# A four-layer selective-scan kernel: delta u B of every fourth state on GpSimd, with B broadcast from DRAM and the decay in PSUM

## The chip, the cores and the metric

One core of one Trainium2 chip. The time is the device time of one launch in microseconds. The engines are called by the profile's names: PE (TensorE), with PEld for its weight loads, DVE (VectorE), ACT (ScalarE), POOL (GpSimd) and SP (SyncE, which here issues the DMAs).

## The reference

Four blocks of a vision state-space model, each `x = x + block(groupnorm(x))`, over 8 images of 48 x 48 positions (L = 2304) and 96 channels. In a block, a projection to 192 channels, a depthwise 3 x 3 convolution and silu give u. u is scanned in four directions (k: along rows, along columns, and both reversed), with 16 states n for each channel:

```
x_dbl = x_proj[k] @ xs[k]                       # -> dts, Bs (16 rows), Cs (16 rows)
delta = softplus(dt_proj[k] @ dts + bias)
dA    = exp(delta * A[n])
h     = dA * h + (delta * u) * B[n]             # a recurrence over the 2304 positions
y     = sum over n of h * C[n],  plus D * u
```

The four directions are summed, layer-normalised, multiplied by silu(z) and projected back to 96 channels. The last block forms the same recurrence from a cumulative sum of log dA, with dB u divided by (decay + 1e-12).

## The kernel before

The 8 images are handled as 4 pairs. The channels of a pair, 2 x 192, fill three tiles of 128 partitions: t = 0 and 1 are the first 128 channels of each image, t = 2 has the last 64 of both. For one layer and pair there are 12 groups (t, ph, d): three tiles, two scan layouts ph (rows, columns), two directions d. `prologue` makes u and the projections, which go to DRAM: `xd` holds the rows of dts, B and C in fp32, `xb` holds B split into three bf16 parts. `prepare` makes delta (`dl`) and delta times u (`du`) of one group, in five pieces. `epilogue` does the norm and the output projection in 16 pieces, `ECHUNKS`.

A group is scanned in three chunks of 768 positions, each with 16 states. One state of one chunk is a unit; the first three layers have 6912 of them. For a unit, class `Chunk` issues:

- `load`: broadcasts C's row of this state from `xd` to all partitions, tile `cb` (7 buffers); with the first state also the bf16 rows `brow`. All DMAs are on SP's queue.
- `decay`: `da = exp(A delta)` on ACT (L543), tile `da`, 4 buffers.
- `spread`: PE multiplies `brow` with a selecting matrix, which puts B's row on all partitions, in a PSUM tile `b` of two buffers (L558).
- `scan`: DVE multiplies `b` by `du` (L570), then scans `h = da * h + b` in place of `da` (L574). ACT keeps the last column for the next chunk (L585), and POOL multiplies C by h in place of `cb` (L586).
- `add_up`: PE adds that to the sum over states in PSUM with an identity matmul (L593); after state 15 `collect` adds the sum to `y`.

The order of the work is written out in `run`, for unit k of the list `todo`: make the next unit ready, scan this one, take one step of the generators that run beside it (`prepare` of the next group, `prologue` of the next pair in the last third of a pair, `epilogue` of the previous pair in the first two thirds), and add up the unit three before:

```
get_ready(k + 1)
c.scan(n)
step(coming)
...
todo[k - LAG][1].add_up(todo[k - LAG][2])      # LAG = 3
```

`get_ready(k)` loads C of unit k + 2 (`LOADS`), makes the decay of unit k + 1 (`DECAYS`) and spreads B of unit k. The framework beneath puts in the semaphores, gives out the buffers of a tile's pool, and may move an instruction ahead of others on its engine where its own timing model has it ready first; so the order on an engine is near the written one, but not it.

The last layer is scanned by class `Edge` on its outer rows alone, four states at a time, by the same calls `load`, `decay`, `spread`, `scan`, `add_up`.

Of the kernel before, what the change touches and what calls it, by code (L numbers as in the profile page):

```python
# [31 lines left out]
F32 = mybir.dt.float32  # L35
# [4 lines left out]
P = 128  # L40
# [3 lines left out]
NS = 16  # L44
# [48 lines left out]
def ss2d_layers_kernel(ctx: ExitStack, tc: tile.TileContext, x_in, consts, weights, out):  # L93
# [7 lines left out]
    ypool = ctx.enter_context(tc.tile_pool(name="y", bufs=1))  # L101
    rpool = ctx.enter_context(tc.tile_pool(name="brow", bufs=2))
    cbpool = ctx.enter_context(tc.tile_pool(name="cb", bufs=7))
    apool = ctx.enter_context(tc.tile_pool(name="da", bufs=4))
    qpool = ctx.enter_context(tc.tile_pool(name="rq", bufs=2))
    capool = ctx.enter_context(tc.tile_pool(name="carry", bufs=2))
    tmp = ctx.enter_context(tc.tile_pool(name="tmp", bufs=3))
# [399 lines left out]
    class Chunk:  # L507


        def __init__(self, l, p, t, ph, d, i, group):  # L510
            self.l, self.p, self.t, self.ph, self.d, self.group = l, p, t, ph, d, group
            self.c0, self.m = SCANS[i if d == 0 else len(SCANS) - 1 - i]
            self.first, self.last = i == 0, i == len(SCANS) - 1
            self.batches = range(2) if t == 2 else (t,)
            self.brow = self.acc = None
            self.cb, self.da, self.rq, self.b, self.h = {}, {}, {}, {}, {}

        def load(self, n):

# [16 lines left out]

        def decay(self, n):

            s, m = state[self.l, self.p], self.m
            dl, _ = s["dd", self.t, self.ph, self.d]  # L540
            da = apool.tile([P, SCAN], F32, name="da", tag="da")[:, :m]
            self.da[n] = da
            nc.scalar.activation(  # L543
                da, dl[:, self.c0 : self.c0 + m], AF.Exp,
                scale=columns_of(self.l, self.t, self.ph, self.d, n),
            )

        def spread(self, n):

            if self.l == NLAYER - 1:  # L550

                self.rq[n] = rq = qpool.tile([P, SCAN], F32, name="rq", tag="rq")[:, : self.m]
                nc.scalar.activation(rq, self.da[n], AF.Ln, bias=decay_eps)
                nc.scalar.activation(rq, rq, AF.Exp, scale=-1.0)
            k, w = picked(self.t, n)
            self.b[n] = b = pb.tile([P, 2 * BANK], F32, name="b", tag="b")
            for z, zm in pieces(self.m):
                nc.tensor.matmul(  # L558
                    b[:, z : z + zm], w, self.brow[:k, z : z + zm], start=True, stop=True
                )  # L560

        def scan(self, n):
            s, m = state[self.l, self.p], self.m
            way = (lambda z: z) if self.d == 0 else (lambda z: z[:, ::-1])
            _, du = s["dd", self.t, self.ph, self.d]
            carries = self.group["carry"]
            start = 0.0 if self.first else carries[:, n : n + 1]
            da, c = self.da.pop(n), self.cb[n][:, :m]
            b = self.b.pop(n)[:, :m]
            nc.vector.tensor_mul(b, du[:, self.c0 : self.c0 + m], b)  # L570
            if self.l < NLAYER - 1:

                h = da
                nc.vector.tensor_tensor_scan(way(h), way(da), way(b), start, ALU.mult, ALU.add)  # L574
# [11 lines left out]
            nc.gpsimd.tensor_mul(c, c, h)  # L586
# [38 lines left out]
    class Edge:  # L625
# [10 lines left out]
        @staticmethod  # L636
        def quad(z, pitch=EDGE):
            return z[:, : QUAD * pitch].rearrange("p (n m) -> p n m", n=QUAD)[:, :, :EDGE]

        def load(self, i):  # L640
            s = state[self.l, self.p]
# [86 lines left out]
    def epilogue(l, p):  # L728
# [110 lines left out]
    def run(pairs, short):  # L839
# [22 lines left out]

        def get_ready(k):

            if k == 0:
                for i in range(LOADS):
                    todo[i][1].load(todo[i][2])
                for i in range(DECAYS):
                    todo[i][1].decay(todo[i][2])
            if k + LOADS < len(todo):  # L870
                todo[k + LOADS][1].load(todo[k + LOADS][2])
            if k + DECAYS < len(todo):
                todo[k + DECAYS][1].decay(todo[k + DECAYS][2])
# [157 lines left out]
```

## Time and profile before

| what | value |
|---|---|
| median of 3 runs | 25,898.13 us (25,891.26 to 25,907.81) |
| profiled run | 25,884.7 us; its span 25,882.9 us |
| granted PE clock, mean | 0.881 |
| DMA | 3150.92 MB, 122 GB/s, 40.2% of 16 engines' span |

A profile is of one execution. In its lines "L570 DVE ... b<-du,b" is line 570 of the kernel, the engine, and the tile written and the tiles read; "x6912 | 6481.8, 951" the count, the busy time in us and the mean of one in ns; then the idle time of the engine just before these instructions, and what ended it ("<-PE b L558 2461.6"). Lines of waits have the waiting instruction, the one that released it, and the time in us in all, the number of times and the longest. The three regular layers take the first 23,700 us of the span, the last layer the rest.

### The profile page before, as it was taken

What the parts mean: (1) busy time and instruction counts of PE and PEld (TensorE: products, weight loads), DVE (VectorE), ACT (ScalarE), POOL (GpSimd) and SP (SyncE); (2) the same over time, 40 slices, a digit from 0 to 9 for tenths busy, and PEclk for the clock granted to TensorE, in tenths of its full rate; (3) what the DMA queues carried; (4) which work ended last, traced back from release to release, by engine and by line L of the source; (5) the groups of instructions that cost most, each with busy time, mean ns of one, the idle gap of its engine ahead of it and who ended that gap; (6) DMA issues with size and microseconds to landing.
All of it is one profiled execution on the core that took longest, in us unless ns stands there. A gap on an engine that the chain in (4) does not pass through costs nothing. (4 is left out here: it accounts for less than half of the span.)

```text
span 25882.9 us, 233918 instructions
## 1 busy us (share of the span) xinstructions
PE 20983.2 (81%) x64962; PEld 9542.0 (37%) x64962; DVE 20922.0 (81%) x18566; ACT 13772.3 (53%) x22878; POOL 15340.0 (59%) x9545
## 2 busy tenths in 40 slices
PE   7787887887887887887887887887887887887886
PEld 2333333333333333333333333333333333334555
DVE  5888888988888988988988988988888988887443
ACT  4454554554554554554554554554554554555775
POOL 4656656656666656656656656656656656655332
PEclk8898898998898898898898998898898998898886
DMA  2344444434434444434434444444434434444221
GB/s 90 126 122 130 132 123 127 134 119 130 134 120 132 135 121 133 134 121 134 134 121 131 134 122 130 134 121 130 134 119 132 134 120 130 132 122 115 64 62 50
DMA packets 1463442, 3150.92 MB, mean 122 GB/s; under 512 B 190832, under 2 KB 563696, under 8 KB 1448944
## 3 DMA queue, kind: packets, MB, share of 16 engines
q1 hardware_dynamic: 1462128, 3135.85, 40.2%
q8 instruction: 525, 8.60, 0.1%
q14 instruction: 789, 6.46, 0.1%
HBM read 2971.05 MB, written 164.07 MB: 121 GB/s over the span
## 5 line engine op out<-in xcount | busy, mean ns | idle before, releaser
L586 POOL TENSOR_TENSOR cb<-cb,da 128x768 f32<-128x768 f32 x6912 | 12427.8, 1809 | 7755.9 <-DVE da L574 4843.6
L593 PE MATMUL acc<-cb,cst 128*128 128x512 f32 (+1 forms) x27648 | 12228.8, 568 | 2394.0 <-POOL cb L586 2114.9
L543 ACT ACTIVATE da<-dl,a 128x768 f32<-128x768 f32 x6912 | 6448.9, 935 | 7878.0 <-POOL cb L586 7851.1
L570 DVE TENSOR_TENSOR b<-du,b 128x768 f32<-128x768 f32 x6912 | 6481.8, 951 | 2488.9 <-PE b L558 2461.6
L574 DVE TENSOR_TENSOR_SCAN da<-da,carry,b 128x768 f32<-128x768 f32 x4608 | 8182.2, 1801 | 90.0 <-ACT da L543 35.4
L593 PEld LDWEIGHTS acc<-cb,cst 128*128 128x128 f32 x27648 | 5323.8, 213 | 7776.8 <-issue 4049.3
L558 PE MATMUL b<-brow,pick 48*128 48x512 bf16 (+3 forms) x13824 | 3721.7, 354 | 1719.3 <-DVE da L574 1637.9
L574 DVE TENSOR_TENSOR_SCAN da<-da,b 128x768 f32<-128x768 f32 x2304 | 3961.5, 1742 | 83.1 <-ACT da L543 54.1
L558 PEld LDWEIGHTS <-pick 48*128 48x128 bf16 (+1 forms) x13824 | 919.9, 98 | 5287.6 <-DVE da L574 3139.0
L585 ACT COPY carry<-da 128x1 f32<-128x1 f32 x4608 | 847.4, 184 | 2226.7 <-DVE da L574 2205.3
L258 PE MATMUL ps<-pad,diag 128*128 128x480 f32 (+1 forms) x4320 | 1799.7, 559 | 60.2 <-ACT u L223 36.3
L461 POOL TENSOR_TENSOR lg<-lg,w 128x480 f32<-128x480 f32 (+2 forms) x768 | 864.8, 1126 | 837.5 <-ACT w L459 753.6
L464 DVE SCALAR_TENSOR_TENSOR ps<-ps,lg 128x480 f32<-128x480 f32 (+2 forms) x768 | 473.9, 617 | 799.3 <-POOL lg L462 756.3
L258 PEld LDWEIGHTS ps<-pad,diag 128*128 128x128 f32 x4320 | 783.2, 191 | 857.9 <-issue 619.9
L444 PE MATMUL ps<-dts,w 6*128 6x480 f32 (+8 forms) x2048 | 933.3, 628 | 73.9 <-DVE du L470 39.5
L744 PE MATMUL ps<-ey,cst 128*128 128x144 f32 (+1 forms) x4096 | 846.9, 334 | 82.4 <-ACT ey L768 66.5
L462 POOL TENSOR_TENSOR lg<-lg,e 128x480 f32<-128x480 f32 (+2 forms) x768 | 863.0, 1124 | 37.3
L745 PE MATMUL ps<-ey,mean 128*128 128x144 f32 (+1 forms) x4096 | 782.7, 315 | 0.0
L744 PEld LDWEIGHTS ps<-ey,cst 128*128 128x128 f32 (+1 forms) x4096 | 511.6, 179 | 364.9 <-issue 185.3
L448 ACT ACTIVATE ps<-ps,w 128x480 f32<-128x480 f32 (+2 forms) x768 | 457.7, 596 | 347.4 <-PE ps L444 346.8
L224 ACT ACT_TABLE_LOAD x496 | 636.4, 1283 | 8.7
L223 ACT ACT_TABLE_LOAD x496 | 636.4, 1283 | 8.2
(118 smaller groups left out, 14292.6 us busy)
## 6 DMA issues: line engine op xcount, KB each, us to landing
cb<-xd SPq DMA_DIRECT2D x4736, 384.0 KB
cb<-xd SPq DMA_DIRECT2D x4736, 192.0 KB
yd<-y SPq DMA_DIRECT2D x48, 1152.0 KB
ey<-yd SPq DMA_DIRECT2D x256, 216.0 KB
brow<-xb SPq DMA_DIRECT2D x576, 72.0 KB
xb<-parts SPq DMA_DIRECT2D x288, 108.0 KB
ex<-xs SPq DMA_DIRECT2D x256, 108.0 KB
xd<-xt SPq DMA_DIRECT2D x32, 684.0 KB
```

Source lines behind the costliest of these rows:

```text
L258: nc.tensor.matmul(ps[:, :m], ly.diag[:, int(t == 2), j, :], pad[:, r0 + dy : r0 + dy + nr, dx : dx + W], start=(j == 0), stop=(j == 8),)
L444: nc.tensor.matmul(o[:, :m], ly.dtw[q0 : q0 + r, k, chans], dts[q0 : q0 + r, :m], start=True, stop=True,)
L461: nc.gpsimd.tensor_sub(lg, lg, w1)
L462: nc.gpsimd.tensor_add(lg, lg, e)
L543: nc.scalar.activation(da, dl[:, self.c0 : self.c0 + m], AF.Exp, scale=columns_of(self.l, self.t, self.ph, self.d, n),)
L558: nc.tensor.matmul(b[:, z : z + zm], w, self.brow[:k, z : z + zm], start=True, stop=True)
L570: nc.vector.tensor_mul(b, du[:, self.c0 : self.c0 + m], b)
L574: nc.vector.tensor_tensor_scan(way(h), way(da), way(b), start, ALU.mult, ALU.add)
L585: nc.scalar.copy(carries[:, n : n + 1], h[:, end : end + 1])
L586: nc.gpsimd.tensor_mul(c, c, h)
L593: nc.tensor.matmul(self.acc[:, z : z + zm], ident, c[:, z : z + zm], start=(n == 0), stop=(n == NS - 1),)
L744: nc.tensor.matmul(o, mean_w[:, cols], z[:, b, :], start=True, stop=False)
```

## The change

In the first three layers, every fourth state (n = 3, 7, 11, 15) becomes a pooled one. For such a unit:

- B's row comes in fp32 from `xd` by a broadcasting DMA, as C's does, into a new SBUF tile `bb` of two buffers. This `load_b` is issued four units ahead (`LOADS + 2`).
- POOL multiplies it by `du` in place (`weigh`), one unit ahead.
- `spread` issues no matmuls. Instead the exp of the decay is made there, and it is written to a PSUM tile of the pool that the others use for B.
- `scan` has no multiplication on DVE; the scan reads the decay from PSUM and `bb` from SBUF and writes h to `bb`, which POOL and ACT then read.

The other units stay as they were. The decay of an unpooled unit is now issued after the spread of the unit before it. `da` has 3 buffers where it had 4, and `ex` and `ey` of the epilogue have one where they had two. `Edge` has `load_b` and `weigh` that do nothing.

```diff
+    bbpool = ctx.enter_context(tc.tile_pool(name="bb", bufs=2))
-    apool = ctx.enter_context(tc.tile_pool(name="da", bufs=4))
+    apool = ctx.enter_context(tc.tile_pool(name="da", bufs=3))
...
+        def pooled(self, n):
+            return n % 4 == 3 and self.l < NLAYER - 1
+
+        def load_b(self, n):
+            if not self.pooled(n):
+                return
+            s, m, at = state[self.l, self.p], self.m, slice(self.c0, self.c0 + self.m)
+            row = 2 * layers[self.l].rank + 2 * NS * self.d + n
+            self.b[n] = b = bbpool.tile([P, SCAN], F32, name="bb", tag="bb")
+            for z in self.batches:
+                o = b[64 * z : 64 * z + 64] if self.t == 2 else b
+                nc.sync.dma_start(
+                    o[:, :m],
+                    s["xd"][self.ph, z, row : row + 1, at].to_broadcast(
+                        [64 if self.t == 2 else P, m]
+                    ),
+                )
+
+        def weigh(self, n):
+            if self.pooled(n):
+                _, du = state[self.l, self.p]["dd", self.t, self.ph, self.d]
+                b = self.b[n][:, : self.m]
+                nc.gpsimd.tensor_mul(b, b, du[:, self.c0 : self.c0 + self.m])
...
         def decay(self, n):
+            if not self.pooled(n):
+                self.exp(n, apool.tile([P, SCAN], F32, name="da", tag="da"))
...
+            if self.pooled(n):
+                self.exp(n, pb.tile([P, 2 * BANK], F32, name="b", tag="b"))
+                return
...
-            nc.vector.tensor_mul(b, du[:, self.c0 : self.c0 + m], b)
+            if not self.pooled(n):
+                nc.vector.tensor_mul(b, du[:, self.c0 : self.c0 + m], b)
             if self.l < NLAYER - 1:
-                h = da
+                h = b if self.pooled(n) else da
                 nc.vector.tensor_tensor_scan(way(h), way(da), way(b), start, ALU.mult, ALU.add)
...
-            x = sm2.tile([DM, 2, EM], F32, name="ex", tag="ex")
+            x = sm1.tile([DM, 2, EM], F32, name="ex", tag="ex")
...
-            y = sm2.tile([P, 3, EM], F32, name="ey", tag="ey")
+            y = sm1.tile([P, 3, EM], F32, name="ey", tag="ey")
...
+            def early(ahead, what):
+                for i in range(0 if k == 0 else k + ahead, min(k + ahead + 1, len(todo))):
+                    getattr(todo[i][1], what)(todo[i][2])
+
+            early(LOADS + 2, "load_b")
+            early(LOADS, "load")
...
                 c.spread(n)
+            early(DECAYS, "weigh")
+            for i in range(max(1, k + DECAYS), min(k + DECAYS + 1, len(todo))):
+                todo[i][1].decay(todo[i][2])
```

More of the change, by code (lines that the diff above doesn't have):

```diff
@@ L515, in __init__ @@
             self.brow = self.acc = None
-            self.cb, self.da, self.rq, self.b, self.h = {}, {}, {}, {}, {}
+            self.cb, self.da, self.rq, self.b = {}, {}, {}, {}
+        def pooled(self, n):
[19 more added lines that the diff above has]
+                nc.gpsimd.tensor_mul(b, b, du[:, self.c0 : self.c0 + self.m])
         def load(self, n):
@@ L537, in decay, with exp @@
         def decay(self, n):
+            if not self.pooled(n):
+                self.exp(n, apool.tile([P, SCAN], F32, name="da", tag="da"))
+        def exp(self, n, da):
             s, m = state[self.l, self.p], self.m
             dl, _ = s["dd", self.t, self.ph, self.d]
-            da = apool.tile([P, SCAN], F32, name="da", tag="da")[:, :m]
-            self.da[n] = da
+            self.da[n] = da = da[:, :m]
             nc.scalar.activation(
@@ L638, in quad, with load_b @@
             return z[:, : QUAD * pitch].rearrange("p (n m) -> p n m", n=QUAD)[:, :, :EDGE]
+        def load_b(self, i):
+            pass
+        weigh = load_b
         def load(self, i):
@@ L863, in get_ready @@
         def get_ready(k):
-            if k == 0:
[L866 to L873, printed above, removed]
+            def early(ahead, what):
[3 more added lines that the diff above has]
+            early(LOADS, "load")
+            if k == 0:
+                todo[0][1].decay(todo[0][2])
             if k < len(todo):
```

## The prediction

> **What bounds the kernel now.** First the page's busy line and the groups, to see which engine carries the scan and what one unit (one state n of one chunk of 768 positions) costs on each engine.
>
> ```profile
> PE 20983.2 (81%) x64962; PEld 9542.0 (37%) x64962; DVE 20922.0 (81%) x18566; ACT 13772.3 (53%) x22878; POOL 15340.0 (59%) x9545
> ...
> L586 POOL TENSOR_TENSOR cb<-cb,da 128x768 f32<-128x768 f32 x6912 | 12427.8, 1809 | 7755.9 <-DVE da L574 4843.6
> ...
> L543 ACT ACTIVATE da<-dl,a 128x768 f32<-128x768 f32 x6912 | 6448.9, 935 | 7878.0 <-POOL cb L586 7851.1
> L570 DVE TENSOR_TENSOR b<-du,b 128x768 f32<-128x768 f32 x6912 | 6481.8, 951 | 2488.9 <-PE b L558 2461.6
> L574 DVE TENSOR_TENSOR_SCAN da<-da,carry,b 128x768 f32<-128x768 f32 x4608 | 8182.2, 1801 | 90.0 <-ACT da L543 35.4
> ...
> L558 PE MATMUL b<-brow,pick 48*128 48x512 bf16 (+3 forms) x13824 | 3721.7, 354 | 1719.3 <-DVE da L574 1637.9
> ```
>
> There are 6912 units: 3 layers, 4 pairs, 12 groups, 3 chunks, 16 states. Averages over the span mix stages, so next the busy times by window. I cut the windows of one pair at the first scan of each group (48 units). Columns: window, its length, busy time of PE, PEld, DVE, ACT, POOL (with counts), PE clock, DMA share, GB/s. Here are groups 0, 1, 6, then 8, 9 and 10.
>
> ```profile
> 10098.85:10253.87 155.02, 130.41 (x417) 58.37 (x416) 138.61 (x121) 84.71 (x143) 97.83 (x61) 0.88 0.46 147
> 10253.87:10407.44 153.57, 126.91 (x416) 56.13 (x416) 139.25 (x122) 86.24 (x143) 95.69 (x57) 0.92 0.43 133
> ...
> 11020.98:11172.22 151.24, 123.00 (x384) 50.97 (x382) 140.54 (x119) 85.77 (x145) 103.14 (x63) 0.94 0.43 131
> ...
> 11331.34:11512.57 181.23, 169.62 (x501) 78.54 (x500) 141.25 (x119) 104.58 (x157) 96.56 (x59) 0.96 0.38 114
> 11512.57:11696.66 184.09, 159.67 (x471) 71.46 (x469) 138.36 (x112) 100.95 (x162) 113.80 (x76) 0.95 0.41 121
> 11696.66:11892.91 196.25, 142.03 (x348) 55.95 (x348) 136.21 (x110) 88.73 (x155) 124.11 (x90) 0.80 0.45 122
> ```
>
> So there are two regimes. Nine groups of twelve (0 to 7 and 11, mean 154.1 us) are VectorE-bound: DVE is busy 138.2 us of 154.1, or 90%, POOL 97.6, PE about 125. In groups 8 to 10 the next pair's prologue runs beside the scan and TensorE (8, 9) or the chain ACT-POOL of the split (10) lengthens the group to 181 to 196 us with DVE at 136 to 141. Third, the waits of DVE and POOL in the eight groups 0 to 7 (1232.5 us):
>
> ```profile
> DVE b L570 <- PE b L558: 98.7, 93, 3.7
> DVE ps L464 <- POOL lg L462: 14.9, 10, 2.8
> ...
> POOL cb L586 <- DVE da L574: 280.7, 152, 5.2
> ```
>
> DVE's idle time there is nearly all one wait: L570 for B, which PE is late in spreading because the two b tiles come free only when scan k-2 ends and PE often still has the matmuls of L593 in front. POOL follows the scan and waits for it: 152 times in 384 units, 1.85 us each.
>
> **What the Trainium skill says.** GPSIMD Engine Reference, 3.1 (Elementwise): a two-input operation of GpSimd takes about twice VectorE's time (1.96 at 2048 elements). The trace agrees: 1809 against 951 ns is 1.90. SBUF — State Buffer, "SBUF: two separate sides": the two engines lock each other out of a shared port pair only where the VectorE operation is in a 2-port mode or has two SBUF inputs. Today L570 and L574 read one tensor from SBUF and one from PSUM, and L586 never stretches (1791 to 1908 ns), which agrees; after the change the pooled scan reads da from PSUM and b from SBUF, again one each, so I charge no lock. PSUM — Partial Sum Buffer, "The four PSUM rules": GpSimd and DMA cannot touch PSUM; no run shows it, but it explains why this B comes from DRAM and not from L558. ScalarE: Activation LUTs, "Step-by-step": a PSUM destination is the faster one for an ACTIVATE. The trace does not show it: at 128x480, L448 writes PSUM in 626 ns and L452 SBUF in 562.
>
> **The change part by part.** Pooled are the units with n % 4 = 3 of the layers before the last: 1728 of 6912, 12 per group.
>
> 1. Removed: 1728 multiplications L570. 1728 x 0.951 = 1643 us of DVE, 11.4 us per group. In the nine DVE-bound groups all of it lies on the bounding engine: 11.4 x 9 x 12 = 1231 us. In groups 8 to 10 it doesn't bound.
> 2. Removed: the two matmuls L558 of these units, 3721.7 / 4 = 930 us of PE, 6.5 us per group. In groups 8 and 9, where PE is busy 169.6 of 181.2 and 159.7 of 184.1, I count it: 6.5 x 2 x 12 = 156 us. In group 10 nothing. With them goes a quarter of the waits of L570: 98.7 / 8 = 12.3 us per group, a quarter is 3.1, over 108 groups 335 us.
> 3. Added: 1728 multiplications on POOL (weigh), priced as L586: 1728 x 1.809 = 3126 us, 21.7 per group. POOL goes to 119.3 us per ordinary group; DVE would be at 126.8 and PE at about 118. POOL is not the longest but is third in a near tie. A weigh stands in POOL's queue ahead of the multiplication L586 of the unit being scanned, so a late one delays that, and behind it the matmuls L593, the b matmuls queued after those, and the next L570. The idle stretches are as long as a weigh (1.85 against 1.81 us) and there are 1.6 of them per four units for one weigh. Bounds: 0 exposed (it fits every time) to 1.81 us each (3126 us). I take 0.4 us, as about half the stretches are shorter than the mean and the excess is then some 0.8: 0.4 x 1728 = 691 us.
> 4. Moved: the exp of pooled units goes from a da buffer to a PSUM b tile; it now waits for scan k-2 instead of for POOL. It has while scan k-1 runs (1.74 to 1.80 us) to do 0.94 us, so DVE need not wait, unless ACT is inside another operation (0.5 to 0.9 us). Queued behind it on ACT are the exps of the next units; pairing the n-th L543 with the n-th L574, an exp ends 7.7 us (median) before its scan, which hides a delay. Its duration is unknown: 0.83 to 1.0 us around L543's, ACT being 53% busy. Taken as nothing; bound 0 to 0.2 us, 0 to 346 us in all. A pooled scan with the operands' memories swapped: between 60 ns less and 60 ns more, plus or minus 104 us; taken as L574.
> 5. Added DMA: 384 KB per pooled unit, 679 MB to 3136, so the share of the DMA engines goes from 40% by 8.7 points to 49%; no bound. 2304 more issues on SP (two each for t = 2) at the 0.444 us median of L533: 1023 us. SP waits 13,844 us for L593 to free cb buffers, which hides it. The load waits for the product of the pooled unit two before it (bb has two buffers, eight units), behind it stand cb loads that need a newer L593 or nearly so; POOL waits only 353 us for cb loads today. Taken as nothing; bound 0 to 200 us.
> 6. da from 4 to 3 buffers: pooled units take none, so an exp still waits for the product four units before; nothing in the scan. In the last layer, which pools none, it is one buffer less. ex and ey from 2 to 1: a next chunk's load waits for the end of this one's use or store. In the first three layers the epilogue's steps are two units (6.8 us) apart and hide it; in the last 2200 us I charge 40 us (0 to 150), an estimate of 0.5 us for each of the 80 chunks there.
>
> Sum against the profiled span: 25,883 - 1231 - 156 - 335 + 691 + 40 = 24,892 us. In groups 8 to 10 I count no quarter of L570's waits beside the 156: their length is PE's or the split's. One gain is still open: POOL's idle stretches come with scan pairs, and what remains of DVE's stalls (9.2 us per group) shrinks when PE's queue is 6.5 us shorter per group; from nothing to the 9.2, I take 1.5 us, 162 us over 108 groups, for 24,730. The profiled run took 25,885 against the median of 25,898, 13 us that I leave inside the range.
>
> **Rivals.**
> - *All hidden.* DVE keeps its 90%: 154.1 x 126.8 / 138.2 = 141.4, 12.7 us less per group, 1372 in all, with the 156 of groups 8 and 9 and the 40 of the end: 25,883 - 1372 - 156 + 40 = 24,395. For it: POOL idles 37% now. Against: three engines then stand at 84 to 90% and wait for each other in turn.
> - *PE's order takes half of it back.* After a pooled unit DVE reaches the next L570 0.95 us sooner while the b tile still comes free at the same scan; PE has 1.8 us for b (0.54) behind a queued L593 (1.77). Paying 0.5 us per pooled unit more, 864 us: about 25,590. For it: this wait is DVE's largest today.
> - *POOL delays the loop: slower.* The mechanism of point 3 at its upper end. Without exposure the gain is 1231 + 156 + 335 + 162 - 40 = 1844 us, so it decides from 1844 / 1728 = 1.07 us exposed per weigh, some 60% of it. At 1.4 us: 25,883 - 1844 + 2419 = 26,458. For it: PE already waits for POOL (122.5 us in these eight groups), and the softplus steps on POOL hold DVE's L464. Against: L593 trails by units, and the exps by 7.7 us.
> - *The change does not reach.* If the pooled order left DVE at today's pace by any wait, no change within 0.2%. The last layer isn't touched in its scan, as said.
>
> **How the numbers follow.** About the forecast (24,500 to 25,200): 0.50. All hidden, below 24,500: 0.20, of it 0.07 below 24,050. Half taken back, 25,200 to 25,846: 0.13. No change: 0.03. Slower: 0.14, of it 0.11 above 25,950. So faster 0.83, same 0.03, slower 0.14, with 0.2% (52 us) as what a measurement here can tell from no change. The range of 24,050 to 25,950 leaves out 0.18.
>
> **What would show it.** Right: L570 at 5184 instructions, the new POOL group at about 1.8 us x1728, ordinary groups of 144 to 146 us, DVE's wait for PE b below 2150 us in all, no new wait of L574 over 300 us. Wrong: scans waiting for ACT (point 4), L593 waiting for POOL by some 1 us per pooled unit more (point 3), L586 or the scan longer than 1.81 and 1.80 us (a lock after all), or POOL waiting for bb loads (point 5).

## The result and the profile after

The change makes the kernel slower: 26,124.67 us median of 4 runs (26,119.82 to 26,146.97), against 25,898.56 of the kernel before (25,891.26 to 25,907.81). The ratio is 1.0089, 95% interval 1.0071 to 1.0106. The forecast was 24,730.

The lines have moved: after's L607 is the multiplication by du (L570 before), L611 the scan (L574), L623 C times h (L586), L594 and L630 the matmuls for B and for the sum (L558, L593), L576 the exp (L543), L468 a step of softplus (L464). New are L534, the load of B, and L546, the weigh. First the page's busy line and groups, as shown of before, with softplus added:

```profile
PE 20533.7 (79%) x61506; PEld 9561.1 (37%) x61506; DVE 19457.3 (74%) x16838; ACT 13581.4 (52%) x22876; POOL 18356.8 (70%) x11273
...
L623 POOL TENSOR_TENSOR cb<-cb,da 128x768 f32<-128x768 f32 x5184 | 9338.8, 1809 | 3440.3 <-DVE da L611 1364.0
...
L607 DVE TENSOR_TENSOR b<-du,b 128x768 f32<-128x768 f32 x5184 | 4858.5, 950 | 2557.4 <-PE b L594 2542.8
L611 DVE TENSOR_TENSOR_SCAN da<-da,carry,b 128x768 f32<-128x768 f32 x3456 | 6170.6, 1803 | 579.8 <-ACT da L576 521.0
L594 PE MATMUL b<-brow,pick 48*128 48x512 bf16 (+3 forms) x10368 | 2875.8, 364 | 2209.9 <-DVE da L611 1613.7
...
L546 POOL TENSOR_TENSOR bb<-bb,du 128x768 f32<-128x768 f32 x1728 | 3131.7, 1812 | 605.5 <-DMA bb<-xd 443.2
...
L611 DVE TENSOR_TENSOR_SCAN bb<-b,carry,bb 128x768 f32<-128x768 f32 x1152 | 2070.6, 1797 | 161.8 <-POOL bb L546 115.5
...
L576 ACT ACTIVATE b<-dl,a 128x768 f32<-128x768 f32 x1728 | 1550.0, 897 | 559.8 <-DVE da L611 551.3
...
L468 DVE SCALAR_TENSOR_TENSOR ps<-ps,lg 128x480 f32<-128x480 f32 (+2 forms) x768 | 478.7, 623 | 1337.0 <-POOL lg L466 1328.0
```

The last of them in before:

```profile
L464 DVE SCALAR_TENSOR_TENSOR ps<-ps,lg 128x480 f32<-128x480 f32 (+2 forms) x768 | 473.9, 617 | 799.3 <-POOL lg L462 756.3
```

The work came off as planned: 1728 multiplications less, DVE's busy time down from 20,922 to 19,457 us, and the multiplications and scans as long as they were, the pooled scan included. PE's matmuls are 2 to 3% longer (L594 364 ns against 354, L630 578 against 568), at a granted clock of 0.855 against 0.881. And the span grew by 262 us, so DVE idles 1,727 us more than before. Four idle times grew or are new: the wait for B's matmuls is no shorter than before with three quarters of the multiplications (2542.8 against 2461.6), ordinary scans now wait for their decay, DVE waits 572 us longer for POOL's softplus step, and the weigh waits for its load.

Next the windows of the pair shown of before, cut at the first scans of the groups: groups 0, 1, 6, then 8, 9, 10, in the same columns.

```profile
10223.88:10370.83 146.95, 122.04 (x380) 56.95 (x379) 127.66 (x108) 80.28 (x137) 118.07 (x72) 0.84 0.59 182
10370.83:10524.27 153.44, 126.05 (x395) 57.20 (x394) 130.78 (x112) 84.16 (x142) 119.12 (x71) 0.88 0.53 166
...
11106.42:11261.84 155.42, 125.79 (x362) 55.96 (x362) 129.01 (x106) 84.42 (x144) 120.25 (x72) 0.85 0.49 160
...
11412.46:11602.36 189.90, 171.15 (x474) 78.11 (x475) 129.79 (x106) 100.45 (x154) 117.51 (x71) 0.94 0.50 135
11602.36:11799.61 197.25, 159.09 (x447) 71.96 (x445) 128.72 (x99) 103.35 (x165) 134.17 (x88) 0.94 0.51 138
11799.61:12018.34 218.73, 150.25 (x324) 58.59 (x324) 125.73 (x98) 89.52 (x155) 145.19 (x102) 0.74 0.51 129
```

DVE's busy time fell by about 10 us in each, as counted, and the windows did not follow: groups 0, 1 and 6 gained 8.1, gained 0.1, and lost 4.2; groups 8 to 10 lost 8.7, 13.2 and 22.5. Over all 12 pairs (first scan to first scan) groups 0 to 7 went from 153.9 to 148.5 us on average, groups 8 to 11 from 182.9, 186.5, 195.9 and 155.5 to 190.2, 199.4, 220.7 and 175.6. That is 5.4 x 8 x 12 = 518 us won and 65.1 x 12 = 781 us lost. Groups 8 to 11 are those of t = 2, where each broadcast takes two transfers of 192 KB.

The waits of DVE and POOL in groups 0 to 7 of this pair (waiting instruction, releaser, us in all, times, longest):

```profile
DVE b L607 <- PE b L594: 89.5, 73, 3.8
POOL cb L623 <- DVE da L611: 80.1, 54, 3.8
DVE ps L468 <- POOL lg L466: 52.2, 28, 4.6
...
POOL bb L546 <- DMA bb<-xd: 25.2, 23, 2.1
```

POOL has less slack: it waited for the scan 280.7 us here before and waits 80.1 now. DVE's wait for POOL's softplus step grew from 14.9 to 52.2. And the weighs stand at the head of POOL's queue 25.2 us, waiting for B to land. The same waits over the whole span:

```profile
DVE b L607 <- PE b L594: 2542.8, 1489, 18.9
...
DVE da L611 <- ACT da L576: 758.4, 342, 6.2
...
POOL bb L546 <- DMA bb<-xd: 443.2, 349, 5.0
```

Before, scans waited 89.5 us for ordinary decays.

### The profile page after: what moved, and what is told of

It reads as the page before. It is cut to its first block, busy times and chain, and to the rows that moved or that the text cites. A ratio compares the mean times of both kernels' runs of the same rounds, so it can differ in the third digit from the quotient of the medians.

```text
span 26145.1 us, 230327 instructions
## 1 busy us (share of the span) xinstructions
PE 20533.7 (79%) x61506; PEld 9561.1 (37%) x61506; DVE 19457.3 (74%) x16838; ACT 13581.4 (52%) x22876; POOL 18356.8 (70%) x11273
## 5 line engine op out<-in xcount | busy, mean ns | idle before, releaser
L630 PE MATMUL acc<-cb,cst 128*128 128x512 f32 (+1 forms) x27648 | 12312.8, 578 | 2360.0 <-POOL cb L623 2014.5
L623 POOL TENSOR_TENSOR cb<-cb,da 128x768 f32<-128x768 f32 x5184 | 9338.8, 1809 | 3440.3 <-DVE da L611 1364.0
L630 PEld LDWEIGHTS acc<-cb,cst 128*128 128x128 f32 x27648 | 5508.5, 218 | 8118.4 <-issue 4653.0
L576 ACT ACTIVATE da<-dl,a 128x768 f32<-128x768 f32 x5184 | 4827.6, 933 | 6168.4 <-POOL cb L623 6148.1
L607 DVE TENSOR_TENSOR b<-du,b 128x768 f32<-128x768 f32 x5184 | 4858.5, 950 | 2557.4 <-PE b L594 2542.8
L611 DVE TENSOR_TENSOR_SCAN da<-da,carry,b 128x768 f32<-128x768 f32 x3456 | 6170.6, 1803 | 579.8 <-ACT da L576 521.0
L594 PE MATMUL b<-brow,pick 48*128 48x512 bf16 (+3 forms) x10368 | 2875.8, 364 | 2209.9 <-DVE da L611 1613.7
L623 POOL TENSOR_TENSOR cb<-cb,bb 128x768 f32<-128x768 f32 x1728 | 3132.5, 1813 | 686.0 <-DVE bb L611 343.8
L546 POOL TENSOR_TENSOR bb<-bb,du 128x768 f32<-128x768 f32 x1728 | 3131.7, 1812 | 605.5 <-DMA bb<-xd 443.2
L611 DVE TENSOR_TENSOR_SCAN da<-da,b 128x768 f32<-128x768 f32 x1728 | 2980.4, 1742 | 268.7 <-ACT da L576 237.4
L594 PEld LDWEIGHTS <-pick 48*128 48x128 bf16 (+1 forms) x10368 | 733.3, 99 | 4967.0 <-DVE da L611 2664.6
L611 DVE TENSOR_TENSOR_SCAN bb<-b,carry,bb 128x768 f32<-128x768 f32 x1152 | 2070.6, 1797 | 161.8 <-POOL bb L546 115.5
L576 ACT ACTIVATE b<-dl,a 128x768 f32<-128x768 f32 x1728 | 1550.0, 897 | 559.8 <-DVE da L611 551.3
L468 DVE SCALAR_TENSOR_TENSOR ps<-ps,lg 128x480 f32<-128x480 f32 (+2 forms) x768 | 478.7, 623 | 1337.0 <-POOL lg L466 1328.0
L611 DVE TENSOR_TENSOR_SCAN bb<-b,bb 128x768 f32<-128x768 f32 x576 | 1002.9, 1741 | 120.0 <-ACT b L576 63.9
## 6 DMA issues: line engine op xcount, KB each, us to landing
cb<-xd SPq DMA_DIRECT2D x4736, 192.0 KB
bb<-xd SPq DMA_DIRECT2D x1152, 192.0 KB
```

What stands on the lines that cost most here:

```text
L546: nc.gpsimd.tensor_mul(b, b, du[:, self.c0 : self.c0 + self.m])
L576: nc.scalar.activation(da, dl[:, self.c0 : self.c0 + m], AF.Exp, scale=columns_of(self.l, self.t, self.ph, self.d, n),)
L594: nc.tensor.matmul(b[:, z : z + zm], w, self.brow[:k, z : z + zm], start=True, stop=True)
L630: nc.tensor.matmul(self.acc[:, z : z + zm], ident, c[:, z : z + zm], start=(n == 0), stop=(n == NS - 1),)
```

## Experiments

Eighteen kernels were run, each beside the kernel before. "g" columns are the mean lengths in us of groups 0 to 7 and of 8 to 11; the ratios are to the runs of before made beside each kernel.

| kernel | median us | ratio to before, 95% | g0-7 | g8 | g9 | g10 | g11 |
|---|---|---|---|---|---|---|---|
| before | 25,898.56 | 1 | 153.9 | 182.9 | 186.5 | 195.9 | 155.5 |
| after | 26,124.67 | 1.0089, 1.0071 to 1.0106 | 148.5 | 190.2 | 199.4 | 220.7 | 175.6 |
| no_weigh | 25,142.9 | 0.9709, 0.9693 to 0.9726 | 139.7 | 188.7 | 196.3 | 215.7 | 172.6 |
| no_bload | 24,304.05 | 0.9385, 0.9369 to 0.9401 | 138.1 | 180.6 | 186.4 | 194.2 | 154.7 |
| weigh_no_load | 24,686.47 | 0.9531, 0.9515 to 0.9547 | 140.1 | 185.5 | 193.8 | 198.5 | 154.1 |
| small_loads | 24,580.14 | 0.9484, 0.9468 to 0.95 | 138.2 | 184.7 | 188.5 | 202.5 | 162.3 |
| unread | 24,565.51 | 0.9492, 0.9476 to 0.9508 | 138.3 | 181.7 | 186.5 | 194.7 | 154.7 |
| weigh_unread | 24,875.88 | 0.9611, 0.9595 to 0.9627 | 139.4 | 187.5 | 195.4 | 197.8 | 153.9 |
| weigh_no_load_tied | 24,958.13 | 0.9639, 0.9623 to 0.9655 | 143.0 | 183.4 | 192.0 | 201.5 | 155.1 |
| tied | 25,913.28 | 1.0004, 0.9995 to 1.0013 | 146.5 | 190.5 | 197.1 | 220.2 | 176.0 |
| plain_groups | 25,597.88 | 0.9883, 0.9867 to 0.99 | 148.5 | 182.0 | 188.9 | 198.9 | 171.0 |
| plain_tied | 25,373.13 | 0.9801, 0.9785 to 0.9817 | 146.6 | 181.6 | 189.0 | 197.4 | 172.6 |
| half_plain | 25,394.05 | 0.9801, 0.9784 to 0.9817 | 147.5 | 180.4 | 189.0 | 196.5 | 164.2 |
| pool_extra | 26,266.62 | 1.0138, 1.0121 to 1.0155 | 156.7 | 181.7 | 189.3 | 199.6 | 155.7 |
| order_only | 25,884.1 | 0.9997, 0.9989 to 1.0006 | 154.4 | 182.2 | 186.5 | 194.3 | 155.5 |
| traffic | 25,928.2 | 1.0012, 1.0004 to 1.002 | 154.5 | 181.6 | 186.1 | 195.0 | 155.2 |
| traffic_small | 25,949.16 | 1.002, 1.0012 to 1.0027 | 154.4 | 182.3 | 186.0 | 195.3 | 155.8 |
| decay_first | 26,287.49 | 1.0154, 1.0137 to 1.0171 | 149.5 | 190.2 | 199.6 | 221.0 | 176.1 |
| three_bb | 26,285.69 | 1.0142, 1.0125 to 1.0159 | 148.4 | 186.9 | 197.2 | 220.5 | 176.2 |
| mid_load | 26,273.35 | 1.0147, 1.013 to 1.0163 | 149.1 | 183.0 | 205.3 | 223.3 | 179.6 |

Many expectations were missed. `no_weigh`, `pool_extra`, `tied`, `small_loads` and `weigh_no_load_tied` fell between the values of two theories, `no_bload` below and `decay_first` above all that was expected of them; `plain_groups` and `plain_tied` came out 2 and 7 us under theirs.

### Is it the weigh on POOL?

The first theory, T1, was the prediction's own third rival: a weigh delays the C h behind it, and the loop waits. `no_weigh` is after without the weigh, so that delta u is missing from the pooled states:

```diff
-                nc.gpsimd.tensor_mul(b, b, du[:, self.c0 : self.c0 + self.m])
+                pass
```

> The changed kernel without the multiplication by delta u of the pooled states (1728 GpSimd operations left out; these states scan B alone). Theory 1, GpSimd's queue (a weigh delays C h, behind it L593 and the next B on PE): the whole gain of the removed VectorE work appears, 24,400 to 24,900 us. Rival 2, the exp in PSUM and the changed order on ACT and PE: the loss stays, 25,900 to 26,150. Rival 3, the 1728 extra broadcasts hold SP and the cb loads: as rival 2.

It gave 25,142.9: the weigh is worth 982 us, or 0.57 us each, but 413 us of the gap to the forecast stay without it, and groups 8 to 11 stay nearly as long as in after. So T1 alone does not explain the loss. From the other side, `pool_extra` is the kernel before with one more POOL multiplication (du by du, to a buffer nobody reads) per fourth unit, held behind a C h:

```diff
+                z = du[:, self.c0 : self.c0 + self.m]
+                with tc.issue_after(last_c[0]):
+                    nc.gpsimd.tensor_mul(scratch[:, : self.m], z, z)
```

> The kernel before with one more 128x768 multiplication on GpSimd for every fourth state (du by du into a scratch tile that nobody reads), placed behind the C h of three states before; ex and ey with one buffer to make room. Nothing is taken off VectorE. Theory 1: slower than before by 0.6 to 1.2 us each, 26,900 to 28,000. Rivals 2 and 3: GpSimd has room, within 150 us of before, 25,900 to 26,050.

It lost 371 us against its own runs of before, 0.21 us for each added multiplication; some 44 us of it lie after the last regular scan, where nothing was added (2,227.3 us there against 2,182.9). POOL's slack hides most of an operation that waits for no load. But the stand-in is shorter than the weigh. A product of du with itself takes 1,467 ns here, and within 1 ns the same in the three kernels below that have it; the weigh, of two tensors, takes 1,812:

```profile
L546 POOL TENSOR_TENSOR scratch<-du 128x768 f32<-128x768 f32 x1728 | 2535.0, 1467 | 0.0
```

`order_only` keeps the change's new order of calls and its single ex and ey, with no pooled unit at all and da at 4 buffers:

```diff
-            return n % 4 == 3 and self.l < NLAYER - 1
+            return False
```

> The changed kernel with no state pooled and da at four buffers: what is left is the new order of decay and spread, and one buffer for ex and ey. If these cost something by themselves (groups 8 to 10, or the epilogue): over 26,000. Otherwise within 50 us of before, 25,850 to 25,950.

No difference: the rewritten `get_ready` costs nothing.

### Where is it lost, and where in POOL's queue does the weigh stand?

In the trace of after the weighs of groups 0 to 7 stand five or six units ahead of their own unit in POOL's queue (about 90% of them), and in 79% of all cases the next C h had its scan done before the weigh ended. `tied` fixes the place: a weigh may only follow the C h of three states before it. `plain_groups` pools no unit of groups 8 to 10 (gi is the group's number), and `plain_tied` does both:

```diff
-            return n % 4 == 3 and self.l < NLAYER - 1
+            return n % 4 == 3 and self.l < NLAYER - 1 and not 8 <= self.gi <= 10
...
-                nc.gpsimd.tensor_mul(b, b, du[:, self.c0 : self.c0 + self.m])
+                with tc.issue_after(last_c[0]):
+                    nc.gpsimd.tensor_mul(b, b, du[:, self.c0 : self.c0 + self.m])
```

> The changed kernel with each weigh held behind the C h that stands last before it in the written order (three states before its own), where the scheduler had put most of them five or six before. Theory 1 in the form that the early place is at fault (waits for the bb load, and overrun scans): 25,000 to 25,600. If only the load on GpSimd counts and not the place: 26,000 to 26,250. Rivals 2 and 3: unchanged, 26,000 to 26,250.

> The changed kernel with pooled states in groups 0 to 7 and 11 alone, not where the next pair's prologue runs (8 to 10). By the windows of the two profiles the changed kernel loses 45 us per pair in these three groups and gains 2.6 us in each other group: if the losses belong to the place, 25,600 to 25,650; if they move on elsewhere, 25,900 or more.

> Pooled states outside groups 8 to 10 alone, and each weigh held behind the C h of three states before. If the two edits add up (298 us for the groups, 1.7 us in each of 108 groups for the tie): 25,380 to 25,480. If the tie helps only where the prologue runs: 25,560 to 25,640.

`tied` won 211 us on after, to no difference from before. `plain_groups` gave back most of what groups 8 to 10 had lost, and `plain_tied` is the best kernel of this study that computes everything: 2.0% faster than before. `half_plain` is `plain_tied` with every eighth state in place of every fourth:

```diff
-            return n % 4 == 3 and self.l < NLAYER - 1 and not 8 <= self.gi <= 10
+            return n % 8 == 7 and self.l < NLAYER - 1 and not 8 <= self.gi <= 10
```

> The run with pooled states outside groups 8 to 10 and tied weighs (25,373), with half of them: n % 8 = 7. If each pooled state is worth the same (517 us for 1296, 0.40 us each): 25,620 to 25,660. If GpSimd's queue makes the second half worth less than the first: 25,350 to 25,600.

The same time: half the pooled states bring all the gain. Group 11 lengthens with the number of pooled units, 155.5, 164.2, 172.6.

### Is it the load?

`no_bload` leaves out weigh and load, and the pooled scan reads du in place of delta u B (B is missing from these states):

```diff
+            self.b[n] = bbpool.tile([P, SCAN], F32, name="bb", tag="bb")
...
+                b = du[:, self.c0 : self.c0 + self.m] if self.pooled(n) else b
```

> The changed kernel without weigh and also without B's broadcast from DRAM (left out: these states scan delta u alone, which lies in SBUF; the decay stays in PSUM). Against the run without weigh, 25,143: if the 1728 loads on SP are what lengthens groups 8 to 10 there by 35 us per pair, 24,650 to 24,800 and these groups as before; if it is the exp that waits for its PSUM tile in ACT's queue, 25,050 to 25,200 and these groups unchanged.

24,304 us, and groups 8 to 11 are as in before or shorter. So pooling itself, with the decay in PSUM, costs these groups nothing; the load costs 25,143 - 24,304 = 839 us even where POOL does no work on it (`no_weigh` scans B, `no_bload` delta u; their scans take the same 1.80 us). Three theories on how were tried. `decay_first` issues the exp of an ordinary unit ahead of the spread again, in case the decays suffer behind the pooled exp; `three_bb` gives bb a third buffer (rq goes to one, which lengthens the last layer by 210 us); `mid_load` loads three units ahead in place of four. In this order:

```diff
+            for i in range(max(1, k + DECAYS), min(k + DECAYS + 1, len(todo))):
+                todo[i][1].decay(todo[i][2])
             if k < len(todo):
...
-    bbpool = ctx.enter_context(tc.tile_pool(name="bb", bufs=2))
+    bbpool = ctx.enter_context(tc.tile_pool(name="bb", bufs=3))
...
-            early(LOADS + 2, "load_b")
+            early(LOADS + 1, "load_b")
```

> The changed kernel with the decay of the next unit written ahead of the spread, as in the kernel before, so that it stands ahead of the pooled exp on ACT. If decays queued behind a pooled exp are the loss in groups 8 to 10: these groups shorten by 10 to 30 us per pair, 25,750 to 26,000. If the scheduler's order follows its own timing and not the written order, or the cause is elsewhere: 26,050 to 26,180.

> The changed kernel with three bb buffers instead of two; rq of the last layer has one instead of two to make room (the last layer may take up to 150 us longer, read apart). If SP's wait for a free bb tile is the cost of the loads: 12 groups of a pair shorter by 40 to 70 us, 25,400 to 25,750. If traffic is the cost: the groups as in the changed kernel within 10 us per pair, 26,050 to 26,300.

> The changed kernel with B loaded three units ahead instead of four, so that the wait for a free tile ends earlier relative to the load and the weigh falls later. SP's queue as the cause: 25,600 to 25,950. Traffic as the cause: 26,050 to 26,350, the weigh now waiting for its load in places.

None helped: the first and the last lost 163 and 149 us more than after, and with the 210 us of the last layer taken off, `three_bb` gained some 50. A third buffer did not free SP's queue: the loads are issued 8.2 units ahead of their scan on average, in place of 5.6, and SP still stood there for 3,078 us (3,604 in after). `three_bb` and `mid_load` fell in the range that their expectations gave to traffic, so the bytes had to be tried by themselves.

`small_loads` is `no_bload` with loads of 48 columns in place of 768, into the same bb buffers:

```diff
-            s, m, at = state[self.l, self.p], self.m, slice(self.c0, self.c0 + self.m)
+            s, m, at = state[self.l, self.p], 48, slice(self.c0, self.c0 + 48)
```

> The run without B's broadcast (24,304; weigh and B left out, delta u scanned alone), with the 1728 loads put back but of 48 columns instead of 768, in the same place and with the same waits for a free bb tile; the scan waits for them and overwrites them. Two causes can make the loads cost 839 us. Traffic on the DMA engines (679 MB): 24,250 to 24,450. SP's queue, held at the load until a bb tile is free, with the cb, dts and xb transfers behind it: 24,950 to 25,200.

Between the two: with a sixteenth of the bytes 276 of the 839 us remain. That does not tell bytes from dependence, because the length of a load may also change the order that the framework lays out. So the bytes alone next: `traffic` is the kernel before with the same 1728 broadcasts into a scratch buffer that nobody reads, `traffic_small` the same with 48 columns:

```diff
+                    nc.sync.dma_start(
+                        o[:, :m],
+                        s["xd"][self.ph, z, row : row + 1, self.c0 : self.c0 + m].to_broadcast(
+                            [64 if self.t == 2 else P, m]
+                        ),
+                    )
```

> The kernel before with only the transfers added: 1,728 further broadcasts of a row of B (384 KB each) on SP's queue into a buffer that nobody reads, four units ahead, and the ex and ey buffers single to make room. Nothing of the computation is left out. Theory 1 (the loads cost by themselves, as traffic and as issues of SP): slower than before by 300 to 850 us, so 26,200 to 26,750 us, with groups 8 to 10 longer by 20 to 45 us a pair in all. Rival (the loads cost only together with the changed order of GpSimd and VectorE's scans out of PSUM): within 100 us of before.

> The same with loads of 48 columns in place of 768 (24 KB), so that SP's issues and waits stay and nearly no bytes move. If the bytes carry the cost, under a third of what the full loads add, at most 280 us over before; if SP's issues carry it, as much as the full loads.

22 and 43 us over before, and some 24 us of each lie after the last regular scan. The bytes and the issues are free there, as step 5 of the prediction had it. But nothing holds such a load, and the framework moved them up: of the 2,303 transfers of `traffic` in the trace, 2,273 were issued in groups 0 to 6. In the pooled kernels the same was tried with `unread` (`no_bload` with the full loads into the scratch buffer) and `weigh_unread` (the same with a weigh that multiplies du by du). `weigh_no_load` has that weigh and no load. All three leave B out of the pooled states; the two with the scratch buffer have one rq, so 210 us come off for a comparison.

```diff
-                o = b[64 * z : 64 * z + 64] if self.t == 2 else b
+                o = scratch[64 * z : 64 * z + 64] if self.t == 2 else scratch
...
-                nc.gpsimd.tensor_mul(b, b, du[:, self.c0 : self.c0 + self.m])
+                z = du[:, self.c0 : self.c0 + self.m]
+                nc.gpsimd.tensor_mul(b, z, z)
```

> After with the weigh kept and the load of B left out: GpSimd multiplies delta u by itself into the bb buffer, so B is missing from the pooled states. It completes the square of weigh and load. If the two costs add, about 25,290 us (25,200 to 25,400). If most of the weigh's cost is its waiting for its load, 24,500 to 25,000. If the load costs only where the weigh is left out, near 26,100.

> The kernel without weigh and without B in the pooled states (as no_bload, 24,304 us), with the full loads of B added into a buffer that nobody reads; rq single to make room, which lengthens the last layer by some 210 us as in three_bb. If the load costs by its bytes in the pooled order: its 839 us come back, about 25,350 us with the 210. If it costs by the dependence on the bb buffers (SP held for a buffer, work ordered around the arrival): 24,500 to 24,600, with the groups as in no_bload (139.9, 180.6, 186.4, 194.2 us).

> The same with the weigh (delta u times delta u, B left out), which waits for no load: weigh_no_load, 24,686 us, with the unread loads and rq single. Bytes as the cost: after's 26,125 and the 210, so 26,200 to 26,350. Dependence as the cost: 24,850 to 25,000.

| us, rq taken off | no load | full load, nobody depends on it | full load into bb |
|---|---|---|---|
| no weigh | 24,304 | 24,356 | 25,143 |
| weigh (stand-in, the real one in the last column) | 24,686 | 24,666 | 26,125 |

Without the weigh, 679 MB more cost 52 us when nobody depends on them, and the same loads cost 839 us when the pooled scans do. With the weigh the load costs up to 1,439 us; "up to", because the 24,686 and 24,666 have the shorter stand-in, and the real weigh is 345 ns longer each, 596 us of POOL time, of which no run shows how much the loop feels. The stand-in costs 382 us, 0.22 each, nearly as in `pool_extra`. `weigh_no_load` fell where it was expected if most of the weigh's cost is its waiting for its load; that the two costs add was refuted.

One thing is not settled by this table. The unread loads do not stand where the loads of after stand: `after` issues 132 to 156 of them in each of groups 0 to 7 (summed over the 12 pairs) and 275 to 297 in each of groups 8 to 11; `unread` issues 187 to 286 in groups 0 to 7 and then 225, 110, 0 and 22. Groups 4, 10 and 11 of one pair of `unread`, then 10 and 11 of the same pair of `no_weigh`:

```profile
8195.12:8328.29 133.17, 113.38 (x394) 52.31 (x394) 128.11 (x108) 85.38 (x146) 98.34 (x59) 0.97 0.68 219
...
9109.90:9301.56 191.66, 137.57 (x324) 55.71 (x324) 125.89 (x97) 88.57 (x155) 124.11 (x90) 0.80 0.47 122
9301.56:9456.91 155.35, 102.52 (x274) 47.26 (x274) 124.40 (x99) 66.76 (x115) 97.36 (x58) 0.84 0.48 136
```

```profile
9374.46:9588.04 213.58, 144.44 (x324) 56.06 (x324) 125.73 (x97) 89.45 (x155) 124.30 (x90) 0.78 0.50 131
9588.04:9761.01 172.97, 113.48 (x274) 50.93 (x274) 125.27 (x99) 67.04 (x115) 97.32 (x58) 0.77 0.54 144
```

So for groups 0 to 8 the bytes are ruled out: `unread` has more of them in groups 0 to 7, up to a DMA share of 0.68, and is as long there as `no_bload` (138.3 against 138.1 us); in group 8 it has three quarters of them, at 181.7 us against 180.6, where `no_weigh` takes 188.7. For groups 9 to 11, where `no_weigh` lost 592 of the 839 us, they are not. There `small_loads` speaks: its loads stand as in after, with a sixteenth of the bytes, and groups 9 to 11 lost 18 us a pair, against 49 with full loads. With nearly no bytes the dependence costs the 18; how the other 31 divide between bytes and a later landing is open.

### Through what does the dependence cost?

SP's own waits, first of after, then of `unread` (its lines: L565 the load of C, L536 the load into the scratch buffer):

```profile
SPq L563 <- PE acc L630: 8537.2, 4370, 15.9
SPq L534 <- POOL cb L623: 2143.1, 1092, 8.6
SPq L286 <- POOL parts L283: 1649.1, 245, 99.1
SPq L534 <- ACT carry L622: 1461.1, 514, 10.4
```

```profile
SPq L565 <- PE acc L633: 10810.1, 5644, 11.7
...
SPq L536 <- DMA scratch<-xd: 409.2, 361, 5.0
```

In after SP stands 3,604 us at loads of B until a bb buffer is free. The Trainium skill has a DMA's semaphore wait done by the issuing sequencer before dispatch, there for GpSimd's path (DMA: Bandwidth & Descriptors, "Anatomy of one DMA — SWDGE (gpsimd) path"); these 3,604 us show the same for SP, and what stands behind such a load on the queue stands too. Most of these holds take the place of holds that the loads of C had: from the issue of a C load to the start of its C h the median is 13.7 us in `no_weigh` and 13.6 in `unread`. But not all. POOL's waits for rows of C, of `no_weigh`, of `unread` and of `small_loads`:

```profile
POOL cb L623 <- DMA cb<-xd: 612.4, 264, 11.0
```

```profile
POOL cb L626 <- DMA cb<-xd: 378.7, 181, 8.7
```

```profile
POOL cb L624 <- DMA cb<-xd: 568.8, 241, 12.8
```

In groups 10 and 11 alone these are 427, 161 and 341 us. With a sixteenth of the bytes the rows of C come nearly as late, so it is the dependence that holds them back.

DVE's waits for ordinary decays, of `no_weigh` and of `unread`:

```profile
DVE da L611 <- ACT da L576: 753.3, 329, 6.7
```

```profile
DVE da L614 <- ACT da L578: 97.5, 89, 4.1
```

All of these 656 us sit in groups 8 to 11, where `no_weigh` lost 689 of the 839. Pairing exps and scans by their tiles shows a different order there. In group 11 a pooled exp stands ahead of the exp of an earlier ordinary unit in 44% of cases (19% in `unread`, 28% in `small_loads`). In `unread` the framework then moved the pooled scan up too, in all 28 cases; in `no_weigh`, `small_loads` and after it did so in none of 64, 40 and 72. There the exp is ahead and its scan is not, and the ordinary exp that is needed first stands behind. A quarter of the ordinary exps of group 11 end 0.3 us or less before their scan (3.6 us in `unread`). That this order is a cause fits the waits but was not tried alone: `decay_first` changed the written order and left this one as it was. And it is a part only. Following each of the 753 us back along ACT's queue, 301 end at the exp itself, which waits for POOL to free its da buffer, 150 at a pooled exp ahead, 144 at a carry copy that waits for the scan before, the rest mainly at steps of `prepare` and `prologue`.

With the weigh, groups 0 to 7 lose as well, 9.1 us each against `weigh_unread`, or 874 us in all, and no ordinary decay is waited for there. Bytes do not explain it, since `weigh_unread` has more loads in these groups than after; the longer weigh is at most 4.1 us of the 9.1 (12 x 0.345). DVE's waits in `weigh_unread` over the whole span:

```profile
DVE b L610 <- PE b L597: 2044.8, 1216, 16.7
DVE ps L470 <- POOL lg L468: 1096.2, 472, 157.4
...
DVE da L614 <- ACT da L579: 158.6, 117, 4.4
```

Against these, after waits 498 us more for B's matmuls, 232 for softplus and 600 for decays. In each of groups 0 to 7 the wait for B is 11.9 us in place of 5.5, and that for softplus 6.3 in place of 4.7.

In POOL's queue, a weigh of `weigh_no_load` stands seven units ahead, right where its buffer comes free, and the C h behind it was ready 0.55 us (mean, at most a weigh's length) before the weigh's end; in after it is 1.17 us. `weigh_no_load_tied` moves it, without a load, behind the C h of three states before:

```diff
-                    nc.gpsimd.tensor_mul(b, z, z)
+                with tc.issue_after(last_c[0]):
+                    nc.gpsimd.tensor_mul(b, z, z)
```

> weigh_no_load (B left out) with each weigh held behind the C h of three states before, about where it stands in after, in place of seven units ahead, right behind the C h that frees its buffer. If the place in GpSimd's queue makes the cost of the weigh, most of the difference between weigh_no_load and after: above 25,000, up to 25,500 us. If what costs is that a weigh waits for its load, within 150 us of 24,686.

+272 us, between the two expectations. This place is that of `tied`, two units ahead, and not that of after, as its expectation had it. So the 1,439 us can be walked in measured steps: 272 us from `weigh_no_load` to `weigh_no_load_tied` (the place), 955 from there to `tied` (the load and the longer weigh, at the same place), 211 from `tied` to after (the earlier place). The last fits the traces: in after, weighs stand at the head of POOL's queue for 240 us while the next C h is ready, in `tied` for 1 us. Another way through the kernels would give other steps.

The granted clock is a part of the loop too. PE's longer matmuls for the sum in after, and in `weigh_unread`:

```profile
L630 PE MATMUL acc<-cb,cst 128*128 128x512 f32 x13824 | 8713.0, 716 | 2360.0 <-POOL cb L623 2014.5 <-DVE y L656 139.0 <-POOL bb L546 80.6
```

```profile
L633 PE MATMUL acc<-cb,cst 128*128 128x512 f32 x13824 | 8322.0, 687 | 1900.7 <-POOL cb L626 1549.4 <-DVE y L659 128.6 <-DVE y L649 65.9
```

The clock was at half in 28% of the regular groups' time in after and in 20% in `weigh_unread`. It goes with PE's idle time: taking the trace of after in stretches of 3.4 us, a stretch at full clock in which PE was busy under 60% was followed by one at half clock in 65% of cases, one over 90% busy in 0.2%. So, as far as this trace shows, what makes PE wait also makes it slower. How much of the loss comes that way no run separates. It is not the whole: `plain_tied` takes 146.6 us for groups 0 to 7 at a clock of 0.87, where before takes 153.9 at 0.89.

## Why the prediction was wrong, step by step

Step 5 is the step that failed. It took the added loads "as nothing; bound 0 to 200 us", because SP's long waits for cb buffers would hide the issues and the DMA engines had room. For issues and bytes that held where they could be tried alone (`traffic` +22 us, `unread` +52). It named that the load waits for the product of the pooled unit two before it, and put that at nothing; what waits for the load in its turn it did not price. Measured: 839 us without the weigh, and with it 26,125 - 24,686 = 1,439 us, the longer weigh included. The test named for it, POOL waiting for bb loads, came out at 443.2 us.

In profiled spans, the whole way from 24,730 to 26,145:

| term | predicted | measured | from |
|---|---|---|---|
| steps 1, 2, 4, 6 and the open gain | -1,844 | -1,576 | `no_bload` 24,307 against 25,883 |
| step 3, the weigh | +691 | +386 | `weigh_no_load` 24,693 against `no_bload`, a stand-in of 1,467 ns |
| step 5, the load | 0 | +1,452 | after 26,145 against `weigh_no_load`, with 345 ns more for each weigh |

The last two rows depend on what is taken away first. In medians, the load costs 839 us and then the weigh 982 (`no_bload`, `no_weigh`, after); some 600 us, the longer weigh among them, come only where both are there, and the table counts them under the load.

- Steps 1 and 2 and the open gain came out right in sum in groups 0 to 7: 154.1 - 11.4 - 3.1 - 1.5 = 138.1 us predicted, 138.1 measured in `no_bload`. That it fits to the tenth is luck: DVE's wait for B fell by 6.8 us a group in place of the 3.1 + 1.5, and its wait for softplus, which no step named, grew by 2.2. They were wrong on where they apply. Group 11 was counted as VectorE-bound, and it hardly moves (155.5 to 154.7), some 180 us; groups 8 and 9 gain 2.3 and 0.1 us in place of 6.5, some 130 us, so TensorE's busy time did not set their length. The two regimes are the tiles t = 0, 1 and t = 2, not the groups with and without a prologue.
- Step 3 was too dear for a weigh that waits for no load, 0.22 us each in place of 0.4, though that is measured on the shorter stand-in. Beside a load to wait for it is 0.57 us each (after against `no_weigh`), still below the 1.07 us from which the rival "POOL delays the loop" would decide. That rival had the sign and a part of the cause; its own test, PE's matmuls for the sum waiting longer for POOL, did not show (2,014.5 us against 2,114.9).
- Step 4 was right on the durations: the exp in PSUM takes 897 ns against 933 in SBUF (here the trace agrees with the faster PSUM destination of the Trainium skill, ScalarE: Activation LUTs, "Step-by-step: what each stage is for"), the pooled scan 1797 against 1803. Its waits were small while no load was there: in `no_bload` pooled scans wait 223 us for their exp, ordinary ones 93. That 7.7 us of lead hide the rest did not hold in after, where ordinary scans wait 758.4 us, all of it in groups 8 to 11.
- Step 6's 40 us did not show: the time after the last regular scan is 2,177.8 us against 2,182.9.
- No lock showed: L623 stays at 1809 ns and the weigh takes 1812.
- Tests that failed: groups of 144 to 146 us (148.5 in groups 0 to 7), DVE's wait for B below 2,150 us (2,542.8), no new wait of the scan above 300 us (758.4).

What could be better still: `plain_tied` pools group 11, which costs it (172.6 - 155.5) x 12 = 205 us, so pooling t = 0 and 1 alone should come to some 25,170 us; this is an estimate from these runs and was not run. Nor was the load on a queue other than SP's.

## What to carry to other kernels

A transfer is not free because its queue has waiting time and the engines have bandwidth: ask what waits for it, in which in-order queue that waiter stands, and what waits behind. A transfer into a buffer whose release hangs on the loop is a part of the loop, and in this case it also changed the order that the framework laid out on engines that never touch the transfer. The test is cheap: put the same bytes into a buffer that nobody reads (here 52 us in place of 839). Then look in the trace where those transfers came to stand, and how long each stand-in takes: here the unread loads had left groups 10 and 11, and the stand-in for the weigh was 345 ns shorter.

## What was not expected of the hardware

A further 679 MB raised the share of SP's queue on the DMA engines from 43.8% in `no_bload` to 52.8% in `unread`, and to 0.68 in single windows of groups 0 to 7, and left those groups within 0.2 us of each other on average, although all transfers share one queue. An operation of 1.47 us on POOL, busy 59% of the span in before, cost 0.21 to 0.22 us when it depended on no load, in two different kernels. POOL multiplied a tensor with itself in 1,467 ns and two tensors in 1,812, at the same 128x768. And the granted clock fell to half after stretches in which PE had been idle, in 65% of cases against 0.2% after busy ones.
